# A two-layer graph attention kernel in which DMAs add up part of each softmax denominator, and the second layer's norms run in whole-chunk steps

## The chip, the cores and the metric

One core of one Trainium2 chip runs the whole kernel in one launch. The metric is device time in microseconds (us) of one execution, lower is better. Five engines matter: TensorE (PE in the profile; PEld is its weight load), VectorE (DVE), ScalarE (ACT), GpSimd (POOL) and SyncE (SP), which here only issues DMAs. Each engine works through its own queue in order; an instruction that waits holds everything behind it on that engine.

## The reference

Input `x` is 8 graphs x 2048 nodes x 64 features in f32, and `adj` is one 2048 x 2048 matrix of 0 and 1 that all graphs share. Two attention layers run over it, and a residual layer norm ends it:

```python
def _gat_layer(h, mask, b):                       # h: [..., N, D]
    scores = einsum('...nd,...md->...nm', h, h)
    scores = where(mask, scores, -1e16)
    return einsum('...nm,...md->...nd', softmax(scores), h) + b

mask = graph + eye(N) > 0
h    = einsum('bnc,hdc->bhnd', x, Wh)             # 4 heads of 64
z    = leaky_relu(cat(_gat_layer(h, mask, bh)), 0.2)
h2   = einsum('bnk,dk->bnd', z, Wo)               # one head of 64
z2   = leaky_relu(_gat_layer(h2, mask, bo), 0.2)
out  = (z2 - mean) * rsqrt(var + 1e-5) * gamma + beta
x    = layernorm(x + out)
```

## The kernel before

`fast_kernel` does all the work. (`general_kernel` stands behind a flag for inputs whose exponentials leave a safe range; it is not executed here.)

**Units, chunks, blocks.** A unit is one attention over two 64-row maps at once (`j` = 0, 1: two heads of one graph in the first layer, two graphs in the second). There are 20 units: 16 of the first layer and 4 of the second. A second-layer unit (`self.second`) comes when the first-layer units that feed it are done: two of them stand in between first-layer units, two come at the end. A unit has `NC` = 4 chunks of `W` = 512 columns, and a chunk has `NB` = 16 blocks `m` of 128 rows. A step `t` of the main loop is one block, so 1,280 steps in all, 1,024 of the first layer and 256 of the second.

**One block.** `scores` makes a 128 x (2 x 512) block of scores on TensorE in PSUM (two buffers), VectorE subtracts the mask from it into an SBUF tile `e`, and ScalarE takes exp in place. Three steps later (`LAG` = 3) `values` multiplies `e` by the features on TensorE, accumulated over the 16 blocks in PSUM tile `o`. Each f32 matmul shows as two MATMUL records in the profile.

**The denominators.** They are the column sums of all 16 `e` blocks of a chunk. `add_up` hands blocks to GpSimd, which adds them to an SBUF tile `acc`, in the order of blocks. The last `DIRECT` blocks (3 in the first layer, 7 in the second) are not added up but kept as they are. So a first-layer chunk has 4 terms (`acc` and 3 blocks), a second-layer chunk 8. `sums` lets TensorE end them: each term is multiplied by a column of ones for `j` = 0 and 1, and half of the terms go to another column group of the array than the other half. ScalarE copies the result (`zsb`), four small DMAs lay it out over partitions (`zt`), `invert` takes the reciprocal on VectorE, and DMAs bring it back as a 128 x 512 tile `z` by way of DRAM (`rd`). `scale` multiplies.

**The norms.** `norm` does the two layer norms of a second-layer chunk in parts 0 to 7. ScalarE copies and squares the result (part 0), VectorE reduces (1), GpSimd takes the power -1/2 and scales, applies gamma and beta and adds x (2, 3), VectorE reduces (4), ScalarE squares the eight groups of 64 columns one by one with an accumulated sum (5), GpSimd takes the power (6), and ScalarE scales the eight groups one by one (7), after which SyncE stores.

**What sets the order.** The order is written out by hand: `steps` is the list of blocks, `jobs` holds what is done after step `t`, and two tables give the step of each late part of a chunk, counted from its first block: `LATE` for the denominators and `NORM` for parts 0 to 7. Pieces of one chunk therefore stand between blocks of the next ones. `slot` hands out 13 SBUF tiles for the `e` blocks; a tile comes free when its readers are done. Tiles of tag `w` (six) hold `oj`, `o5`, `zsb`, `z`, `sq`; tag `y` (three) holds the norms' `y` and `xr`.

Of the kernel before, what the change touches and what calls it, by code (L numbers as in the profile page):

```python
# [24 lines left out]
F32 = mybir.dt.float32  # L29
# [3 lines left out]
AF = mybir.ActivationFunctionType  # L33
OP = mybir.AluOpType
AX = mybir.AxisListType
# [320 lines left out]
def fast_kernel(ctx: ExitStack, tc: tile.TileContext, x, adj, Wh, bh, Wo, bo, gamma, beta, out, flag):  # L356

    nc = tc.nc
    B, N, C = x.shape
    H, D, _ = Wh.shape  # L360
    P = 128
    NB = N // P
    W = 512
# [14 lines left out]
    dram = ctx.enter_context(tc.tile_pool(name="scratch", bufs=4, space=bass.MemoryType.DRAM))  # L378
# [11 lines left out]
    def wtile(name):  # L390
        return work.tile([P, W], F32, tag="w", name=name)

    def ytile(name):
        return work.tile([P, W], F32, tag="y", name=name, bufs=3)


    ident = const.tile([P, P], F32, name="ident")
# [12 lines left out]
    shifts = const.tile([P, 4], F32, name="shifts")  # L410
# [4 lines left out]
    mhalf = const.tile([P, K], F32, name="mhalf")  # L415
# [94 lines left out]
    class Unit:  # L510


        def __init__(self, n, bp, b2, hp):
            self.n, self.bp, self.b2, self.hp = n, bp, b2, hp
            self.second = hp is None
            self.terms, self.zt, self.z, self.O = {}, {}, {}, {}

        def prepare(self, h):

# [33 lines left out]
        def add_up(self, c, m, e):  # L553

            if m == 0:
                self.terms[c] = [e]
            elif m == 1:
                acc = accs.tile([P, 2, W], F32, tag="acc", name=f"acc{self.n}_{c}")
                nc.gpsimd.tensor_tensor(acc, self.terms[c][0], e, OP.add)  # L559
                self.terms[c] = [acc]  # L560
            elif m < NB - DIRECT[self.second]:
                acc = self.terms[c][0]
                nc.gpsimd.tensor_tensor(acc, acc, e, OP.add)  # L563
            else:
                self.terms[c].append(e)


        def join(self, c):
# [41 lines left out]
        def invert(self, c):  # L610
            n = self.n
            k = n * NC + c
            nc.vector.tensor_reduce(zall[:, k, :], self.zt.pop(c).rearrange("p s k -> p k s"), AX.X, OP.add)
            rt = small.tile([P, 8], F32, tag="rt", name=f"rt{n}_{c}")
            nc.vector.reciprocal(rt, zall[:, k, :])
            rd = dram.tile([2, W], F32, tag="rd", name=f"rd{n}_{c}")
            nc.sync.dma_start(out=rd.rearrange("j (p k) -> (j p) k", k=8), in_=rt)
            self.z[c] = wtile(f"z{n}_{c}")
            for j in range(2):
                nc.sync.dma_start(out=self.z[c][j * D:(j + 1) * D, :], in_=rd[j].partition_broadcast(D))  # L620

# [32 lines left out]
        def norm(self, c, part):  # L654
            if not self.second:
                return
            n = self.n
            v = lambda t: t.rearrange("p (k d) -> p k d", d=D)
            row = lambda t: t.unsqueeze(1).to_broadcast([P, K, D])
            col = lambda t: t.unsqueeze(2).to_broadcast([P, K, D])  # L660
            if part == 0:
                self.y = ytile(f"y{n}_{c}")
                nc.scalar.copy(self.y, self.O[c][0])
                self.sq = wtile(f"sq{n}_{c}")
                nc.scalar.square(self.sq, self.O[c][0])
                self.xr = ytile(f"xr{n}_{c}")
                xv = self.xr.rearrange("p (i b d) -> p i b d", b=2, d=D)
                for b2 in range(2):
                    nc.sync.dma_start(out=xv[:, :, b2, :],
                                      in_=x[2 * self.bp + b2, c * W:(c + 1) * W, :].rearrange("(i p) d -> p i d", p=P))  # L670
                return
            y, xr = self.y, self.xr
            if part == 1:
                self.st = small.tile([P, 6, K], F32, tag="st", name=f"st{n}_{c}", bufs=2)
                nc.vector.tensor_reduce(self.st[:, 0, :], v(self.sq), AX.X, OP.add)
            st = self.st
            if part == 2:
                nc.scalar.activation(st[:, 1, :], st[:, 0, :], AF.Identity, bias=shifts[:, 3:4], scale=1.0 / D)  # L678
                nc.gpsimd.tensor_tensor(st[:, 0, :], st[:, 1, :], mhalf, OP.pow)  # L679
                nc.gpsimd.tensor_tensor(v(y), v(y), col(st[:, 0, :]), OP.mult)  # L680
            elif part == 3:
                nc.gpsimd.tensor_tensor(v(y), v(y), row(gam), OP.mult)
                nc.gpsimd.tensor_tensor(v(y), v(y), row(bet), OP.add)
                nc.gpsimd.tensor_tensor(y, y, xr, OP.add)
            elif part == 4:
                nc.vector.tensor_reduce(st[:, 2, :], v(y), AX.X, OP.add)
            elif part == 5:
                nc.scalar.mul(st[:, 3, :], st[:, 2, :], -1.0 / D)
                for k in range(K):
                    nc.scalar.activation(v(xr)[:, k, :], v(y)[:, k, :], AF.Square, bias=st[:, 3, k:k + 1], scale=1.0,  # L690
                                         accum_out=st[:, 4, k:k + 1])
            elif part == 6:
                nc.scalar.activation(st[:, 5, :], st[:, 4, :], AF.Identity, bias=shifts[:, 3:4], scale=1.0 / D)
                nc.gpsimd.tensor_tensor(st[:, 0, :], st[:, 5, :], mhalf, OP.pow)  # L694
                nc.gpsimd.tensor_tensor(st[:, 1, :], st[:, 3, :], st[:, 0, :], OP.mult)  # L695
            elif part == 7:
                for k in range(K):
                    nc.scalar.activation(v(xr)[:, k, :], v(y)[:, k, :], AF.Identity, bias=st[:, 1, k:k + 1],  # L698
                                         scale=st[:, 0, k:k + 1])
                yv = xr.rearrange("p (i b d) -> p i b d", b=2, d=D)  # L700
# [48 lines left out]
    for i, k in enumerate(range(done, len(pieces) + AHEAD + 1)):  # L749
# [1 line left out]
    xst = {}  # L751


    LATE = [(19, "join"), (20, "join2"), (20, "sums"), (21, "fifth"), (22, "leaky"), (24, "invert"), (28, "scale"), (30, "project"),
            (31, "keep")]
    NORM = [31, 32, 33, 35, 40, 41, 43, 46]
    es = {}
    for t in range(total + 64):
        if t < total:
            u, c, m = steps[t]  # L760
            es[t] = u.scores(c, m)
            if m == 0:
# [5 lines left out]
                n = u.n + 1  # L768
                if n < len(units):
                    v = units[n]  # L770
# [13 lines left out]
        if 0 <= t - LAG < total:  # L784
            u, c, m = steps[t - LAG]
            e = es.pop(t - LAG)
# [57 lines left out]
```

## Time and profile before

| | |
|---|---|
| three runs | 2678.69 us median (2677.74 to 2680.65) |
| profiled execution | 2678.89 us, of which 2677.1 us from the first to the last instruction (the span) |
| TensorE clock granted, mean | 0.985 |
| TensorE busy | 2580.8 us (96%) |
| GpSimd busy | 2265.1 us (85%) |
| VectorE busy | 1832.5 us (68%) |
| ScalarE busy | 1783.3 us (67%) |
| DMA | 55.40 MB, a mean of 21 GB/s |

A busy share is an average over stages with different limits, so the stages are looked at one by one. A row of the timeline gives start, duration, engine, line, operation, tiles (out<-in) and how many instructions are merged in it; in square brackets stands the time that the engine sat idle before it and what ended the wait. A row of a group gives line, engine, operation, tiles, shape and count, then total busy us and mean ns of one, then idle us before them. L563 is line 563 of the kernel before.

### The profile page before, as it was taken

How to read it: one execution, taken by the hardware profiler on the slowest of the kernel's cores; microseconds unless marked ns; L12 is line 12 of the kernel's file. 1: busy time of each engine (PE TensorE's matmuls, PEld its weight loads, DVE VectorE, ACT ScalarE, POOL GpSimd, SP SyncE). 2: the span in 40 equal slices, each digit the busy share in tenths (PEclk: the TensorE clock that was granted, in tenths of full speed). 3: DMA queues.
4: the chain of work that ended last, by engine and by line, in shares of the span. 5: the costliest groups of instructions: out<-in, count | busy, mean ns of one | idle time of the engine just before them, and what ended most of it. 6: DMA issues, size and time to landing. Idle time of an engine off the chain costs nothing.

```text
span 2677.1 us, 54824 instructions
## 1 busy us (share of the span) xinstructions
PE 2580.8 (96%) x23174; PEld 896.5 (33%) x23174; DVE 1832.5 (68%) x1797; ACT 1783.3 (67%) x2089; POOL 2265.1 (85%) x1041
## 2 busy tenths in 40 slices
PE   7999999999999999999999899999999999999993
PEld 3333333333333233333333233333333333333331
DVE  5876776677766577667776667767776777766662
ACT  5766666666667666666667766666666666666774
POOL 5889999899688999889967989988998999967774
PEclk9999999999999999999999999999999999999996
DMA  5300001000001001000001000100000000000011
GB/s 143 125 25 10 9 9 25 10 14 10 13 17 25 9 14 25 10 10 10 10 14 25 21 9 10 25 9 14 9 9 10 10 10 13 10 13 17 21 25 29
DMA packets 118304, 55.40 MB, mean 21 GB/s; under 512 B 91266, under 2 KB 107714, under 8 KB 118050
## 3 DMA queue, kind: packets, MB, share of 16 engines
q1 hardware_dynamic: 117250, 51.36, 7.2%
q8 instruction: 183, 3.00, 0.5%
q0 software_dynamic: 176, 0.26, 0.1%
q14 instruction: 71, 0.58, 0.1%
q10 hardware_dynamic: 624, 0.20, 0.0%
HBM read 46.60 MB, written 4.52 MB: 19 GB/s over the span
## 4 chain that ended last, share of the span: by engine, by line
PE 76%; POOL 11%; ACT 6%; DVE 3%; issue 3%; DMA 0%; SPq 0%; POOLq 0%; DVEq 0%; ACTq 0%
PE s L537 34%; PE o L550 33%; POOL acc L563 6%; PE pz L597 5%; ACT e L541 3%; DVE e L540 2%; PE pn L527 1%; ACT xr L698 1%; PE o L641 1%; ACT xr L690 1%; POOL acc L559 1%; POOL st L694 1%; POOL st L679 1%; ACT hT L508 1%; PE pm L484 1%
## 5 line engine op out<-in xcount | busy, mean ns | idle before, releaser
L540 DVE TENSOR_TENSOR e<-s,mask 128x1024 f32<-128x1024 f32 x1280 | 1562.6, 1222 | 721.7 <-PE s L537 700.3
L563 POOL TENSOR_TENSOR acc<-acc,e 128x1024 f32<-128x1024 f32 x816 | 1933.5, 2369 | 81.2 <-ACT e L541 20.2
L541 ACT ACTIVATE e<-e,shifts 128x1024 f32<-128x1024 f32 x1280 | 1465.1, 1148 | 762.5 <-DVE e L540 748.4
L550 PE MATMUL o<-e,hN 64*64 64x512 f32 x10240 | 1336.6, 592 | 20.2 <-ACT e L541 20.1
L537 PE MATMUL s<-hT 64*64 64x512 f32 x8192 | 1074.3, 595 | 9.6 <-DVE e L540 4.5
L550 PEld LDWEIGHTS o<-e,hN 64*64 64x64 f32 x10240 | 390.9, 134 | 738.6 <-issue 540.7
L537 PEld LDWEIGHTS s<-hT 64*64 64x64 f32 x8192 | 295.8, 133 | 582.2 <-issue 424.9
L559 POOL TENSOR_TENSOR acc<-e,e 128x1024 f32<-128x1024 f32 x80 | 189.3, 2367 | 139.5 <-ACT e L541 139.2
L537 PE MATMUL s<-h2T 64*64 64x512 f32 x2048 | 273.1, 604 | 15.7 <-DVE e L540 15.6
L597 PE MATMUL pz<-e,ones 128*32 128x512 f32 x1216 | 182.1, 600 | 0.0
L679 POOL TENSOR_TENSOR st<-st,mhalf 128x8 f32<-128x8 f32 x16 | 26.3, 1641 | 127.3 <-ACT st L678 127.3
L537 PEld LDWEIGHTS s<-h2T 64*64 64x64 f32 x2048 | 75.2, 135 | 157.9 <-issue 121.3
L597 PE MATMUL pz<-acc,ones 128*32 128x512 f32 x320 | 85.0, 610 | 0.1
L600 ACT COPY zsb<-pz 128x512 f32<-128x512 f32 x80 | 46.7, 584 | 48.3 <-PE pz L597 48.3
L698 ACT ACTIVATE xr<-y,st 128x64 f32<-128x64 f32 x128 | 44.1, 426 | 42.8 <-POOL st L695 42.8
L597 PEld LDWEIGHTS pz<-e,ones 128*32 128x32 f32 x1216 | 41.0, 110 | 68.5 <-issue 68.5
L585 DVE TENSOR_TENSOR o<-o,o 128x512 f32<-128x512 f32 x80 | 55.8, 698 | 5.2 <-ACT o L581 5.2
L624 DVE TENSOR_TENSOR z<-o,z 128x512 f32<-128x512 f32 x80 | 54.5, 681 | 6.0 <-DMA z<-rd 5.7
L577 DVE TENSOR_TENSOR o<-o,oj 128x512 f32<-128x512 f32 x80 | 55.9, 698 | 2.4 <-ACT oj L572 1.0
L485 DVE CAST mask<-pm 128x1024 uint8<-128x1024 bf16 x32 | 39.1, 1223 | 18.5 <-PE pm L484 16.6
L581 ACT ACTIVATE o<-o 128x512 f32<-128x512 f32 x80 | 46.2, 577 | 0.0
L572 ACT COPY oj<-o 128x512 f32<-128x512 f32 x80 | 45.6, 569 | 0.4
(74 smaller groups left out, 681.8 us busy)
## 6 DMA issues: line engine op xcount, KB each, us to landing
z<-rd SPq DMA_DIRECT2D x160, 128.0 KB, 2.9
adj<-in_adj_dram SPq DMA_DIRECT2D x32, 512.0 KB, 4.8
zt<-zsb SPq DMA_DIRECT2D x320, 2.0 KB, 1.8
x<-in_x_dram SPq DMA_DIRECT2D x16, 256.0 KB, 4.6
xr<-in_x_dram SPq DMA_DIRECT2D x32, 128.0 KB, 2.7
out_dram<-xr SPq DMA_DIRECT2D x32, 128.0 KB, 2.1
rd<-rt SPq DMA_DIRECT2D x80, 4.0 KB, 1.4
ws<-in_L_gnn_Wh_dram ACTq DMA_DIRECT2D x2, 64.0 KB, 4.6
```

Of the source, the lines that this page charges most:

```text
L537: nc.tensor.matmul(ps[k * 64:(k + 1) * 64, j, :], self.hT[rows, m * P + k * 64:m * P + (k + 1) * 64], self.hT[rows, c * W:(c + 1) * W], st ...
L540: nc.vector.tensor_tensor(e, ps, mask[c][:, m, :].unsqueeze(1).to_broadcast([P, 2, W]), OP.subtract)
L541: nc.scalar.activation(e, e, AF.Exp, bias=shifts[:, 1:2] if self.second else shifts[:, 0:1], scale=1.0)
L550: nc.tensor.matmul(self.O[c][r][j * D:(j + 1) * D, :], self.hN[rows, m, j * D:(j + 1) * D], e[rows, j, :], start=(m == 0), stop=(m == NB - 1))
L559: nc.gpsimd.tensor_tensor(acc, self.terms[c][0], e, OP.add)
L563: nc.gpsimd.tensor_tensor(acc, acc, e, OP.add)
L577: nc.vector.tensor_tensor(b, b, self.t, OP.add)
L585: nc.vector.tensor_tensor(b, b, self.t, OP.max)
L597: nc.tensor.matmul(pz[q:q + 32, :W], ones, terms[s * half + k][:, j, :], start=(k == 0), stop=(k == half - 1), tile_position=(0, q))
L624: nc.vector.tensor_tensor(dst, self.O[c][1], self.z[c], OP.mult)
L679: nc.gpsimd.tensor_tensor(st[:, 0, :], st[:, 1, :], mhalf, OP.pow)
L698: nc.scalar.activation(v(xr)[:, k, :], v(y)[:, k, :], AF.Identity, bias=st[:, 1, k:k + 1], scale=st[:, 0, k:k + 1])
```

## The change

`add_up` no longer gives all blocks to GpSimd's adder. By the table `CHAINS`, some blocks are added by DMAs issued from GpSimd's queue that read a block and add it onto an earlier block in SBUF (`accum_op=OP.add`). In a first-layer chunk, blocks 3, 6, 9 and 12 are added one after the other onto block 0 (five blocks in one term). In a second-layer chunk, blocks 4, 8, 12 go onto block 0 and blocks 6, 10, 14 onto block 2. GpSimd adds the others into `acc`, now the last blocks too, except block 15 of a second-layer chunk, which stays alone. That leaves 2 terms in the first layer and 4 in the second.

The norms become ten parts: the second norm uses the steps of the first one (GpSimd subtracts the mean, ScalarE squares a whole chunk, VectorE reduces, GpSimd takes the power and scales) in place of the sixteen small ScalarE instructions. `LATE` and `NORM` move most parts by one step or more, and `sums` from behind `join2` to behind `fifth`. Tag `w` has three tiles, `y` four, and `z` gets two of its own.

```diff
-    DIRECT = (3, 7)
+    CHAINS = (((0, 3, 6, 9, 12),), ((0, 4, 8, 12), (2, 6, 10, 14)))
+    ALONE = ((), (15,))
-    work = ctx.enter_context(tc.tile_pool(name="work", bufs=6))
+    work = ctx.enter_context(tc.tile_pool(name="work", bufs=3))
...
         def add_up(self, c, m, e):
             if m == 0:
-                self.terms[c] = [e]
-            elif m == 1:
+                self.terms[c], self.first, self.acc = [], {}, None
+            for k, chain in enumerate(CHAINS[self.second]):
+                if m == chain[0]:
+                    self.first[k] = e
+                    self.terms[c].append(e)
+                    return
+                if m in chain:
+                    nc.gpsimd.dma_start(out=self.first[k], in_=e, accum_op=OP.add)
+                    return
+            if m in ALONE[self.second]:
+                self.terms[c].append(e)
+            elif self.acc is None:
+                self.acc = e
+            elif len(self.terms[c]) == len(CHAINS[self.second]):
                 acc = accs.tile([P, 2, W], F32, tag="acc", name=f"acc{self.n}_{c}")
-                nc.gpsimd.tensor_tensor(acc, self.terms[c][0], e, OP.add)
-                self.terms[c] = [acc]
-            elif m < NB - DIRECT[self.second]:
-                acc = self.terms[c][0]
-                nc.gpsimd.tensor_tensor(acc, acc, e, OP.add)
+                nc.gpsimd.tensor_tensor(acc, self.acc, e, OP.add)
+                self.acc = acc
+                self.terms[c].append(acc)
             else:
-                self.terms[c].append(e)
+                nc.gpsimd.tensor_tensor(self.acc, self.acc, e, OP.add)
...
             elif part == 5:
-                nc.scalar.mul(st[:, 3, :], st[:, 2, :], -1.0 / D)
-                for k in range(K):
-                    nc.scalar.activation(v(xr)[:, k, :], v(y)[:, k, :], AF.Square, bias=st[:, 3, k:k + 1], scale=1.0,
-                                         accum_out=st[:, 4, k:k + 1])
+                nc.scalar.mul(st[:, 4, :], st[:, 3, :], -1.0 / D)
+                nc.gpsimd.tensor_tensor(v(y), v(y), col(st[:, 4, :]), OP.add)
             elif part == 6:
-                nc.scalar.activation(st[:, 5, :], st[:, 4, :], AF.Identity, bias=shifts[:, 3:4], scale=1.0 / D)
-                nc.gpsimd.tensor_tensor(st[:, 0, :], st[:, 5, :], mhalf, OP.pow)
-                nc.gpsimd.tensor_tensor(st[:, 1, :], st[:, 3, :], st[:, 0, :], OP.mult)
-            elif part == 7:
-                for k in range(K):
-                    nc.scalar.activation(v(xr)[:, k, :], v(y)[:, k, :], AF.Identity, bias=st[:, 1, k:k + 1],
-                                         scale=st[:, 0, k:k + 1])
+                self.sq = wtile(f"sr{n}_{c}")
+                nc.scalar.square(self.sq, y)
...
-    NORM = [31, 32, 33, 35, 40, 41, 43, 46]
+    NORM = [32, 33, 34, 36, 42, 43, 45, 46, 47, 50]
```

Parts 7 and 8 are now the reduce of part 1 and the power and scale of part 2 again, and part 9 stores. Three places show how instructions move. A name such as `e_1_3_1873` is block 3 of chunk 1 (the last number only tells buffers apart); names in brackets are what the instruction waits for: `DMASW` is a DMA issued by GpSimd, `DMAHW` one issued by SyncE, the others are engines.

GpSimd's queue in a first-layer chunk, before: one add for each block.

```order
L559 TENSOR_TENSOR acc_1_1902<-e_1_0_1843,e_1_1_1855 128x1024 [waits Activation_49]
L563 TENSOR_TENSOR acc_1_1902<-acc_1_1902,e_1_2_1867 128x1024 [waits Activation_49,Pool_49]
L563 TENSOR_TENSOR acc_1_1902<-acc_1_1902,e_1_3_1879 128x1024 [waits Activation_49,Pool_49]
L563 TENSOR_TENSOR acc_1_1902<-acc_1_1902,e_1_4_1895 128x1024 [waits Activation_49,Pool_49]
L563 TENSOR_TENSOR acc_1_1902<-acc_1_1902,e_1_5_1926 128x1024 [waits Activation_49,Pool_49]
```

The same queue and chunk now.

```order
L573 TENSOR_TENSOR acc_1_1909<-e_1_1_1847,e_1_2_1860 128x1024 [waits Activation_49]
L565 DMA e_1_0_1834<-e_1_3_1873 128x1024 [waits DMAHW1_49,DMAHW2_49,PE_49,Activation_49]
L577 TENSOR_TENSOR acc_1_1909<-acc_1_1909,e_1_4_1889 128x1024 [waits Activation_49,Pool_49]
L577 TENSOR_TENSOR acc_1_1909<-acc_1_1909,e_1_5_1902 128x1024 [waits Activation_49,Pool_49]
L565 DMA e_1_0_1834<-e_1_6_1930 128x1024 [waits DMASW1_49,Activation_49]
L577 TENSOR_TENSOR acc_1_1909<-acc_1_1909,e_1_7_1944 128x1024 [waits Activation_49,Pool_49]
L577 TENSOR_TENSOR acc_1_1909<-acc_1_1909,e_1_8_1957 128x1024 [waits Activation_49,Pool_49]
L565 DMA e_1_0_1834<-e_1_9_1970 128x1024 [waits DMASW2_49,Activation_49]
```

Every third block is a DMA, and from the second one on it waits in GpSimd's queue for the landing of the one before it, two adds earlier.

TensorE's queue where it ends the denominators of a first-layer chunk (`pz`), before.

```order
L597 MATMUL pz_0_2903<-acc_0_2662,ones 32x512 x2
L597 MATMUL pz_0_2903<-e_0_14_2815,ones 32x512 x2
L597 MATMUL pz_0_2903<-e_0_13_2802,ones 32x512 x2
L597 MATMUL pz_0_2903<-e_0_15_2828,ones 32x512 x2
L537 MATMUL s_1_5_2919<-hT_1_2100 64x512 x4
```

The same place now.

```order
L552 MATMUL o_1_1_2867<-e_1_2_2850,hN_2352 64x512
L609 MATMUL pz_0_2903<-e_0_0_2588,ones 32x512 x2
L609 MATMUL pz_0_2903<-acc_0_2663,ones 32x512 x2
L539 MATMUL s_1_6_2915<-hT_1_2091 64x512 x4
L552 MATMUL o_1_0_2866<-e_1_3_2863,hN_2352 64x512
```

Four of eight matmuls are gone, and the place is one block later (before `s_1_6` instead of `s_1_5`).

ScalarE's queue at the end of a second-layer chunk's norms, before (`st`, `xr`, `y` of chunk 0 between the exponentials of chunk 2).

```order
L693 ACTIVATE st_0_6093<-st_0_6093,shifts 128x8 [waits Activation_49]
L541 ACTIVATE e_2_12_6300<-e_2_12_6300,shifts 128x1024 [waits DVE_49]
L541 ACTIVATE e_2_13_6313<-e_2_13_6313,shifts 128x1024 [waits DVE_49]
L541 ACTIVATE e_2_14_6325<-e_2_14_6325,shifts 128x1024 [waits DVE_49]
L698 ACTIVATE xr_0_6078<-y_0_6074,st_0_6093 128x64 [waits Pool_49]
L698 ACTIVATE xr_0_6078<-y_0_6074,st_0_6093 128x64 x7
L541 ACTIVATE e_2_15_6351<-e_2_15_6351,shifts 128x1024 [waits DVE_49]
```

The same place now.

```order
L700 ACTIVATE st_0_6049<-st_0_6049 128x8
L543 ACTIVATE e_2_12_6240<-e_2_12_6240,shifts 128x1024 [waits DVE_49]
L543 ACTIVATE e_2_13_6253<-e_2_13_6253,shifts 128x1024 [waits DVE_49]
L704 ACTIVATE sr_0_6261<-y_0_6045 128x512 [waits Pool_49]
L543 ACTIVATE e_2_14_6269<-e_2_14_6269,shifts 128x1024 [waits DVE_49]
L543 ACTIVATE e_2_15_6283<-e_2_15_6283,shifts 128x1024 [waits DMASW1_49,DVE_49,Activation_49]
L690 ACTIVATE st_0_6049<-st_0_6049,shifts 128x8
```

ScalarE still waits for GpSimd once per chunk, now at one squaring (`sr`), and behind one short GpSimd step instead of behind the power.

More of the change, by code (lines that the diff above doesn't have):

```diff
@@ L393, in ytile @@
     def ytile(name):
[L394 removed]
+        return work.tile([P, W], F32, tag="y", name=name, bufs=4)
     ident = const.tile([P, P], F32, name="ident")
@@ L751, in fast_kernel @@
     xst = {}
-    LATE = [(19, "join"), (20, "join2"), (20, "sums"), (21, "fifth"), (22, "leaky"), (24, "invert"), (28, "scale"), (30, "project"),
-            (31, "keep")]
-    NORM = [31, 32, 33, 35, 40, 41, 43, 46]
+    LATE = [(19, "join"), (20, "join2"), (21, "fifth"), (21, "sums"), (22, "leaky"), (25, "invert"), (29, "scale"), (31, "project"),
+            (32, "keep")]
+    NORM = [32, 33, 34, 36, 42, 43, 45, 46, 47, 50]
     es = {}
```

25 lines of the change are left out of this document (13 added, 12 removed).

## Prediction

> **What bounds the kernel now.** I read the page's busy shares first, then TensorE by stage, then the chain of waits, then the groups by line.
>
> ```profile
> span 2677.1 us, 54824 instructions
> PE 2580.8 (96%) x23174; PEld 896.5 (33%) x23174; DVE 1832.5 (68%) x1797; ACT 1783.3 (67%) x2089; POOL 2265.1 (85%) x1041
> PE 76%; POOL 11%; ACT 6%; DVE 3%; issue 3%; DMA 0%; SPq 0%; POOLq 0%; DVEq 0%; ACTq 0%
> ```
>
> The stages, as busy times in windows (start:end, length, then busy us of each engine, granted clock, DMA share, GB/s):
>
> ```profile
> core 0: us, PE busy (x) PEld busy (x) DVE busy (x) ACT busy (x) POOL busy (x), PEclk, DMA share, GB/s
> 40.00:140.00 100.00, 99.96 (x948) 37.01 (x940) 86.57 (x80) 78.44 (x75) 84.54 (x43) 1.00 0.39 120
> 300.00:640.00 340.00, 339.74 (x3072) 116.38 (x3068) 239.89 (x233) 226.39 (x221) 309.06 (x131) 1.00 0.06 13
> 737.00:900.00 163.00, 149.42 (x1312) 50.44 (x1304) 99.89 (x102) 114.29 (x203) 140.44 (x74) 0.97 0.08 19
> 1390.00:1555.00 165.00, 151.25 (x1328) 51.11 (x1324) 101.90 (x104) 115.12 (x202) 143.12 (x75) 0.97 0.08 19
> 2420.00:2640.00 220.00, 202.72 (x1748) 68.80 (x1740) 132.43 (x137) 152.34 (x285) 165.22 (x92) 0.95 0.09 23
> ```
>
> In a first-layer stage (300 to 640) TensorE has no idle time, at full clock: what leaves its queue there shortens the run, as long as GpSimd, busy 309 of 340 us, doesn't become the limit. In the three second-layer stages TensorE idles 13.6, 13.8 and 17.3 us and its clock falls to 0.97 and 0.95. Why, the timeline of one such place shows:
>
> ```profile
> 875.33 1.65 POOL L694 TENSOR_TENSOR st<-st,mhalf 128x8 f32<-128x8 f32 x1
> 877.29 2.76 ACT L698 ACTIVATE xr<-y,st 128x64 f32<-128x64 f32 x8 [6.34 <-POOL st L695]
> 879.95 2.17 ACT L541 ACTIVATE e<-e,shifts 128x1024 f32<-128x1024 f32 x2
> 881.14 1.56 PE L550 MATMUL o<-e,hN 64*64 64x512 f32 x8 [4.94 <-ACT e L541]
> ```
>
> ScalarE stood 6.3 us before the norm's last scaling, since GpSimd reached the power (L694) late, behind its adds. The exponentials queued behind it came late, and TensorE waited 4.9 us, then ran its eight records in 1.56 us where 1.04 is usual (below).
>
> **The change, part by part.**
>
> *TensorE ends fewer terms.* The two groups of `pz` count 1,536 records, 16 in each of 64 first-layer chunks and 32 in each of 16 second-layer chunks.
>
> ```profile
> L597 PE MATMUL pz<-e,ones 128*32 128x512 f32 x1216 | 182.1, 600 | 0.0
> L597 PE MATMUL pz<-acc,ones 128*32 128x512 f32 x320 | 85.0, 610 | 0.1
> 1330.83 1.46 PE L597 MATMUL pz<-e,ones 128*32 128x512 f32 x10
> 1332.21 1.09 PE L537 MATMUL s<-h2T 64*64 64x512 f32 x8
> 1333.12 1.04 PE L550 MATMUL o<-e,hN 64*64 64x512 f32 x8
> 1333.98 1.04 PE L537 MATMUL s<-h2T 64*64 64x512 f32 x8
> ```
>
> They become 8 and 16, so 768 go. A mean of 600 ns is no price, since records overlap; from start to start, eight take 1333.98 - 1333.12 = 0.86 us, 0.107 each, and a block of 16 takes 1.72. The ten `pz` records above took 1.38 us, 0.138 each, with the change of tile shape, which stays. So 768 x 0.107 = 82 us (by the other price 106), nearly all where TensorE never idles. I take 82.
>
> *GpSimd.* Per first-layer chunk 12 adds become 10 adds and 4 DMA issues, per second-layer chunk 8 become 6 and 6.
>
> ```profile
> 997.75 12.16 POOL L563 TENSOR_TENSOR acc<-acc,e 128x1024 f32<-128x1024 f32 x5
> 1.64 0.74 POOL L454 DMA_DIRECT2D bhb<-in_L_gnn_bh_dram  x1
> 3.97 0.53 POOL L458 DMA_DIRECT2D bet<-in_L_gnn_beta_dram  x1
> ```
>
> An add takes 12.16/5 = 2.43 us, so ten take 24.3. The only DMAs that GpSimd issues before cost it 0.53 to 0.74 us each; each has 128 rows, as the new ones have, so I take 0.65 = d, with bounds 0.5 and twice 0.74 (two operands). The chunk is then 24.3 + 2.6 = 26.9 us of GpSimd. TensorE's chunk: 131 adds in 340 us are 10.9 chunks of 31.1 us, less 0.86 is 30.3; the shortest, 16 x 1.72 and 0.9, is 28.4. GpSimd has room in both.
>
> *The new wait.* DMA k+1 of a chain waits, in GpSimd's queue, for the landing of DMA k; in between stand two adds (4.86 us). If issue to landing takes L, the chunk costs GpSimd 24.3 + d + 3 max(d, L - 4.86); behind the waiting DMA stand all later adds, and `sums` on TensorE waits for the last of them. This stays under 30.3 us up to L = 6.6, and eats up all that the change gains at L = 7.2. No row shows an accumulating transfer. The nearest:
>
> ```profile
> adj<-in_adj_dram SPq DMA_DIRECT2D x32, 512.0 KB, 4.8
> zt<-zsb SPq DMA_DIRECT2D x320, 2.0 KB, 1.8
> z<-rd SPq DMA_DIRECT2D x160, 128.0 KB, 2.9
> bhb<-in_L_gnn_bh_dram POOLq DMA_DIRECT2D x1, 128.0 KB, 4.9
> bet<-in_L_gnn_beta_dram POOLq DMA_DIRECT2D x1, 32.0 KB, 9.1
> ```
>
> `adj` moves as many bytes over as many partitions, so 4.8 is the lower bound. `zt`, within SBUF, has hardly any bytes; 4.8 - 1.8 = 3.0 is then the moving, and twice that for two operands gives 7.8, the upper bound. GpSimd's own DMAs land later (4.9 for 128 KB where SyncE's `z` takes 2.9; 9.1 for the last in line), but in the loading at the start. I take L = 5.5, `adj` and d, nearest to the row of its size: then GpSimd waits for nothing in the first layer. The Trainium skill, in DMA: Bandwidth & Descriptors, "Anatomy of one DMA — SWDGE (gpsimd) path", has 2.0 us and bytes / 436 GB/s for a DMA from GpSimd; my estimate from it is 3.2 us for 512 KB, less than `adj` took here, and by it the 7 us below that I charge for late landings would go.
>
> *What the transfers disturb.* 352 of them, 512 KB each. In window 40 to 140, at a DMA share of 0.39, TensorE is busy 99.96 of 100, so its cost is none. The way of `z` is tighter:
>
> ```profile
> 1024.65 1.10 SPq L620 DMA_DIRECT2D z<-rd  x2
> 1029.61 0.68 DVE L624 TENSOR_TENSOR z<-o,z 128x512 f32<-128x512 f32 x1
> ```
>
> The second is issued at 1025.2 and lands 2.9 later; VectorE uses it 1.5 us after that. If sharing queues doubled the landing, it would be 1.4 us late 80 times, of which 0.5 lies in VectorE's slack per block (1.72 against 1.22): 72 us. Between 0 and 72 I take 5, since the row gives room for half as long again. Slots: a chunk's first block is held to step 21, so two of 13 at most, where three last blocks were held; eight blocks or more (14 us) pass before a transfer's source is written again. Cost none. Tag `w` with three tiles: a fourth is asked for 14 steps after the first, long after its reader; in the mask's stage ScalarE may wait for it, 0 to 10 us, I take none.
>
> *The norms.* GpSimd's part of a chunk, by these rows:
>
> ```profile
> L679 POOL TENSOR_TENSOR st<-st,mhalf 128x8 f32<-128x8 f32 x16 | 26.3, 1641 | 127.3 <-ACT st L678 127.3
> L680 POOL TENSOR_TENSOR y<-y,st 128x512 f32<-128x512 f32 x16 | 16.7, 1042 | 1.3
> L684 POOL TENSOR_TENSOR y<-y,xr 128x512 f32<-128x512 f32 x16 | 20.4, 1274 | 1.3
> L540 DVE TENSOR_TENSOR e<-s,mask 128x1024 f32<-128x1024 f32 x1280 | 1562.6, 1222 | 721.7 <-PE s L537 700.3
> L698 ACT ACTIVATE xr<-y,st 128x64 f32<-128x64 f32 x128 | 44.1, 426 | 42.8 <-POOL st L695 42.8
> ```
>
> Two powers (1.64), three of 1.04 (scale twice, subtract the mean) and three of 1.28, with gaps 10.8 us, where it was 9. A second-layer chunk takes 6 x 2.43 + 6 x 0.65 + 10.8 = 29.3 us of GpSimd, TensorE 16 x 1.72 + 1.7 + 1.1 (the centring matmuls) = 30.3: it fits, and GpSimd alternates adds and issues where it ran eight adds on end, so ScalarE's one wait (`sr`) should find it in time. What was lost there before: 44.6 us idle and, by the clocks (0.03 x 328 + 0.05 x 220 = 21, of which I count 13, as some of it lies in the idle time), 58 in all. What is late next: block 14's DMA is issued some 5 us before TensorE reaches `sums`, so 0.6 us in each of 12 chunks, 7. And twice, norms of a second-layer unit run in two first-layer chunks, which need 24.3 + 2.6 + 10.8 = 37.7 us of GpSimd against 30.3: 2 x 7.4, less 3 us that `sums` has in hand, is 12, twice 24. So 58 - 31 = 27 gained, between -10 and 58. SyncE's queue has the same DMAs, the store three steps later; nobody waits for it before the end. At the end the tail gets 2 us shorter (half the `pz`, two groups of eight like L698's 2.76 us gone, one wait for block 14 more), between -4 and +3.
>
> **The sum.** The profiled execution took 2678.89 us, 1.8 more than its span and 0.2 over the median of the runs (2678.69). 2678.9 - 82 - 27 - 2 + 5 = 2573.
>
> **The rivals.**
>
> A, slower: the adding transfer takes 7.2 us or more, and GpSimd's chain is the bound. For it speaks that it reads two operands and that GpSimd's DMAs landed latest of all; against it that `adj` at 4.8 was measured in the busiest stage of the DMA queues. At 7.8 the chunk is 24.3 + 0.65 + 8.8 = 33.8, 3.5 over 30.3, x 64 = 224: 2797. At 7.5 it is 2737. The Trainium skill, in Collectives: The Full Stack, "The bandwidth ceiling: the fold count and why AG ≠ RS ≠ AR", says that an adding transfer pushes two reads through one read ring and gets half the rate of a copy. That is this case's mechanism; no run here shows it yet.
>
> B, slower: the issue itself costs GpSimd over 1.9 us (24.3 + 4d = 32.0). At three times the 0.74 row it gives 33.2, 2.9 x 64 = 186: 2759. Against it: two to three times any row.
>
> C, less gained: the waits only move. The norms' stalls come back as waits for the last landing, and `z` comes late: 2573 + 27 + 67 = 2667, down to 2630 for half of it. For it speaks the 1.5 us in hand; against it that GpSimd no longer runs eight adds on end.
>
> D, no change: TensorE isn't short of time where `pz` stands. Against it stands 339.74 of 340.
>
> **How the numbers follow.** This kernel's runs spread by 0.1%, so 0.2% is about what can be told from no change. Forecast 0.58 (2540 to 2630: from all 58 us of stalls gained to `z` half late), C 0.12, D 0.04, A 0.20, B 0.06. Faster is the forecast and C, 0.70; same is D, 0.04; slower is A and B, 0.26. The likeliest is 2573. For 8 in 10 the range goes from 2540 to 2740, up to L = 7.5: half of A, most of B and a little below are left out. Within the forecast alone it is 2540 to 2630.
>
> **What would show it.** `pz` groups with 768 records in all; `add` groups with 736; in window-like first-layer stages TensorE still without idle time and GpSimd busy under 95%. The issue of an accumulating DMA under 0.8 us, its landing under 6.6. In the second layer, idle time of TensorE about half of what it was, and ScalarE's wait before `sr` under 2 us. Wrong would be: GpSimd idle before its DMA with the DMA as releaser, 64 x 3 times; TensorE waiting for `acc` or for the chain's block at `pz`; a granted clock under 0.98 in the first layer, which an idle TensorE would bring; VectorE waiting at L624's place for `z`.

## The result, and the profile after

The change made the kernel faster: 2605.49 us median (2604.9 to 2612.93, 4 runs) against 2678.22 of the kernel before beside it (2676.3 to 2680.65, 4 runs), a ratio of 0.9734, 95% interval 0.9715 to 0.9754. That is 73 us, where 106 were forecast. A second set of runs gave 0.9725 (0.9711 to 0.9738). The span of the profiled execution is 2604.0 us.

The page of the changed kernel, its busy shares and its chain of waits:

```profile
span 2604.0 us, 53831 instructions
...
PE 2507.1 (96%) x22406; PEld 866.4 (33%) x22406; DVE 1834.2 (70%) x1813; ACT 1703.5 (65%) x1721; POOL 2214.6 (85%) x1249
...
PE 67%; DMA 9%; POOL 5%; DVE 5%; issue 3%; ACT 3%; SPq 1%; DVEq 0%; ACTq 0%; POOLq 0%
```

768 matmul records are gone, but DMA, which had 0% of the chain before, now has 9%. The windows, at the same kinds of place as before (the loading, a first-layer stretch, the three second-layer stretches; their places moved with the shorter span):

```profile
core 0: us, PE busy (x) PEld busy (x) DVE busy (x) ACT busy (x) POOL busy (x), PEclk, DMA share, GB/s
40.00:140.00 100.00, 95.28 (x873) 34.48 (x872) 81.30 (x75) 75.07 (x71) 78.49 (x47) 0.97 0.72 178
300.00:640.00 340.00, 336.24 (x3012) 114.03 (x3008) 241.25 (x235) 227.18 (x223) 295.41 (x154) 1.00 0.42 81
730.00:890.00 160.00, 149.66 (x1320) 51.36 (x1312) 107.48 (x113) 101.97 (x117) 146.33 (x91) 0.98 0.47 92
1370.00:1530.00 160.00, 151.61 (x1324) 51.16 (x1320) 107.93 (x112) 101.97 (x115) 148.89 (x93) 0.98 0.47 94
2370.00:2580.00 210.00, 190.89 (x1696) 67.89 (x1688) 141.59 (x151) 131.22 (x157) 186.52 (x128) 0.96 0.59 117
```

TensorE, which had no idle time in the first layer (339.74 of 340) and none in the loading (99.96 of 100), now idles 3.8 and 4.7 us there, at DMA shares of 0.42 and 0.72 where 0.06 and 0.39 were. Groups of instructions show for what:

```profile
L577 POOL TENSOR_TENSOR acc<-acc,e 128x1024 f32<-128x1024 f32 x656 | 1605.5, 2447 | 129.8 <-ACT e L543 104.7
...
L565 POOL DMA_DIRECT2D e<-e x352 | 320.7, 911 | 48.6 <-ACT e L543 25.4
...
L609 PE MATMUL pz<-e,ones 128*32 128x512 f32 x448 | 100.1, 610 | 10.1 <-DMA e<-e 7.2
L636 DVE TENSOR_TENSOR z<-o,z 128x512 f32<-128x512 f32 x80 | 54.9, 687 | 72.1 <-DMA z<-rd 72.0
L609 PE MATMUL pz<-acc,ones 128*32 128x512 f32 x320 | 85.0, 610 | 9.4 <-POOL acc L577 9.4
...
e<-e POOLq DMA_DIRECT2D x352, 512.0 KB, 4.9
z<-rd SPq DMA_DIRECT2D x160, 128.0 KB, 3.6
adj<-in_adj_dram SPq DMA_DIRECT2D x32, 512.0 KB, 7.8
zt<-zsb SPq DMA_DIRECT2D x320, 2.0 KB, 1.8
```

The accumulating DMA itself is no bottleneck: 0.91 us of GpSimd to issue, 4.9 us to landing. But `z` lands in 3.6 us where 2.9 was, and VectorE waits 72 us for it at the scale (L636), 40 times. Before, the row of the scale was:

```profile
L624 DVE TENSOR_TENSOR z<-o,z 128x512 f32<-128x512 f32 x80 | 54.5, 681 | 6.0 <-DMA z<-rd 5.7
```

One such wait in the timeline of the changed kernel:

```profile
603.51 0.69 DVE L636 TENSOR_TENSOR z<-o,z 128x512 f32<-128x512 f32 x1 [2.48 <-DMA z<-rd]
...
604.12 2.34 DVE L542 TENSOR_TENSOR e<-s,mask 128x1024 f32<-128x1024 f32 x2
605.36 2.33 ACT L543 ACTIVATE e<-e,shifts 128x1024 f32<-128x1024 f32 x2 [3.09 <-DVE e L542]
605.38 1.09 PE L539 MATMUL s<-hT 64*64 64x512 f32 x8 [1.36 <-DVE e L542]
```

VectorE stands 2.48 us before the scale; the mask's subtraction (L542) queued behind it is late, so the score buffers come free late, and TensorE idles 1.36 us.

Where the 73 us lie, by stretches of the span. Each stretch is cut where ScalarE copies a chunk's sums (`zsb`); "start" is the time to the first score matmul, when the kernel only loads. One profiled execution each, in us:

| stretch (chunks) | before | changed | chains alone | norms alone | gap | gap+later | relief | mixed |
|---|---|---|---|---|---|---|---|---|
| start | 28.7 | 25.7 | 29.6 | 29.9 | 30.4 | 29.7 | 27.4 | 31.6 |
| loading (first 4) | 151.1 | 158.9 | 156.2 | 151.1 | 152.3 | 151.8 | 152.2 | 152.5 |
| first layer, three stretches (56) | 1753.0 | 1727.3 | 1727.4 | 1753.0 | 1715.0 | 1714.5 | 1716.4 | 1716.5 |
| second layer, first place (6) | 211.5 | 200.2 | 204.7 | 214.0 | 206.2 | 200.6 | 194.6 | 196.5 |
| second layer, second place (6) | 211.4 | 202.5 | 201.3 | 214.6 | 202.1 | 200.0 | 191.8 | 192.9 |
| second layer, at the end (8) | 282.2 | 252.0 | 258.4 | 280.9 | 253.8 | 255.3 | 262.1 | 255.0 |
| tail | 39.2 | 37.4 | 39.6 | 38.1 | 38.1 | 37.9 | 42.4 | 42.9 |

The columns behind "changed" are the experiments below (the profiled execution of "gap" was 8 us over its median). In the first layer, the time from the first `pz` record to the next other matmul, added up, fell from 103.8 to 55.8 us, 48.0, though the stretch got only 25.7 shorter.

### The profile page after: what moved, and what is told of

It is laid out like the page before. It is cut to its first block, busy times and chain, and to the rows that moved or that the text cites. A ratio compares the mean times of both kernels' runs of the same rounds, so it can differ in the third digit from the quotient of the medians.

```text
span 2604.0 us, 53831 instructions
## 1 busy us (share of the span) xinstructions
PE 2507.1 (96%) x22406; PEld 866.4 (33%) x22406; DVE 1834.2 (70%) x1813; ACT 1703.5 (65%) x1721; POOL 2214.6 (85%) x1249
## 3 DMA queue, kind: packets, MB, share of 16 engines
q0 software_dynamic: 50864, 184.83, 37.8%
## 4 chain that ended last, share of the span: by engine, by line
PE 67%; DMA 9%; POOL 5%; DVE 5%; issue 3%; ACT 3%; SPq 1%; DVEq 0%; ACTq 0%; POOLq 0%
PE s L539 32%; PE o L552 29%; DVE e L542 4%; DMA z<-rd 4%; PE pz L609 3%; POOL acc L577 3%; DMA rd<-rt 2%; DMA e<-e 2%; DMA zt<-zsb 1%; PE pn L529 1%; ACT e L543 1%; PE o L653 1%; POOL st L691 1%; SPq L618 1%; POOL y L692 1%
## 5 line engine op out<-in xcount | busy, mean ns | idle before, releaser
L542 DVE TENSOR_TENSOR e<-s,mask 128x1024 f32<-128x1024 f32 x1280 | 1558.8, 1221 | 588.6 <-PE s L539 566.6
L577 POOL TENSOR_TENSOR acc<-acc,e 128x1024 f32<-128x1024 f32 x656 | 1605.5, 2447 | 129.8 <-ACT e L543 104.7
L539 PEld LDWEIGHTS s<-hT 64*64 64x64 f32 x8192 | 289.9, 133 | 611.5 <-issue 378.5
L565 POOL DMA_DIRECT2D e<-e x352 | 320.7, 911 | 48.6 <-ACT e L543 25.4
L609 PE MATMUL pz<-e,ones 128*32 128x512 f32 x448 | 100.1, 610 | 10.1 <-DMA e<-e 7.2
L636 DVE TENSOR_TENSOR z<-o,z 128x512 f32<-128x512 f32 x80 | 54.9, 687 | 72.1 <-DMA z<-rd 72.0
L691 POOL TENSOR_TENSOR st<-st,mhalf 128x8 f32<-128x8 f32 x32 | 56.9, 1777 | 41.6 <-ACT st L690 41.4
L531 DVE TENSOR_TENSOR hN<-pn,bhb 128x1024 f32<-128x1024 f32 x32 | 39.1, 1223 | 8.6 <-PE pn L529 7.8
```

The costliest lines, as they stand in the source:

```text
L539: nc.tensor.matmul(ps[k * 64:(k + 1) * 64, j, :], self.hT[rows, m * P + k * 64:m * P + (k + 1) * 64], self.hT[rows, c * W:(c + 1) * W], st ...
L542: nc.vector.tensor_tensor(e, ps, mask[c][:, m, :].unsqueeze(1).to_broadcast([P, 2, W]), OP.subtract)
L565: nc.gpsimd.dma_start(out=self.first[k], in_=e, accum_op=OP.add)
L577: nc.gpsimd.tensor_tensor(self.acc, self.acc, e, OP.add)
L609: nc.tensor.matmul(pz[q:q + 32, :W], ones, terms[s * half + k][:, j, :], start=(k == 0), stop=(k == half - 1), tile_position=(0, q))
L636: nc.vector.tensor_tensor(dst, self.O[c][1], self.z[c], OP.mult)
```

## The experiments

**What each half of the change is worth.** The first kernel has the chains with the norms of before (`norm` as it was, `NORM = [32, 33, 34, 36, 41, 42, 44, 47]`); the second has the new norms without the chains:

```diff
-    CHAINS = (((0, 3, 6, 9, 12),), ((0, 4, 8, 12), (2, 6, 10, 14)))
-    ALONE = ((), (15,))
+    CHAINS = ((), ())
+    ALONE = ((13, 14, 15), (9, 10, 11, 12, 13, 14, 15))
```

> The denominators' part alone; the norms are the kernel before's, with their parts one step later as the rest of the table asks. Theory: the norms' new steps gave about 16 us, read from the end of the kernel (the two last second-layer units became 30.2 us shorter, of which 8 chunks x 1.72 us are the missing pz records), and nothing in the two second-layer units in the middle; so this kernel takes 2605 + 16 = 2621 us (2613 to 2632), and the waits of ScalarE for GpSimd's st are back (over 25 us). Rival 1, the prediction's size: the norms gave 27 to 58 us, so 2632 or more. Rival 2: the chain's shorter rows of adds cured the norm stalls by themselves, so the norms' edit gave nothing: 2605.

> The norms' part alone (with the new late tables and tiles); the denominators are summed as before, 4 and 8 terms, no accumulating DMA, sums back at step 20. Theory: the norms' edit gives about 16 us, so 2662 us (2652 to 2670); z lands in 2.9 us again, adj in 4.8, and VectorE waits under 10 us for z, because no transfer disturbs them. Rival 1: the late tables, not the transfers, made z late: VectorE's waits for z stay above 40 us here too. Rival 2: the norm steps need the lighter GpSimd queue of the chains, and with eight adds on end the norms are no faster: 2678.

Chains alone: 2614.4 us, 0.9753 (0.9739 to 0.9766). Norms alone: 2684.53 us against 2681.2, 1.0014 (1.0005 to 1.0023): no gain, and 1 to 6 us lost. So the theory failed for the second kernel, and its second rival held. The first kernel's time lies in its theory's range (2613 to 2632), but the sign of that theory, waits of over 25 us, did not come. ScalarE's waits for GpSimd, in three rows from the waits of norms alone, chains alone and the changed kernel (line awaited, total us, times, longest):

```profile
ACT sr L704 <- POOL y L701: 79.4, 16, 9.0
```
```profile
ACT xr L710 <- POOL st L707: 9.4, 4, 3.0
```
```profile
ACT sr L704 <- POOL y L701: 12.4, 6, 5.9
```

In the kernel before that wait was 42.8 us. The new norms give GpSimd one step more (the mean), and behind eight adds on end they make ScalarE wait 79.4. The chains cure the wait by themselves: 9.4 us with the old norms. Between chains alone (0.9753) and the changed kernel (0.9734 and 0.9725) lie 5 to 8 us, which the norms' edit adds to them. And with the late tables of the change, but no transfers (only `sums` is back at step 20), `z` is not late in norms alone:

```profile
L636 DVE TENSOR_TENSOR z<-o,z 128x512 f32<-128x512 f32 x80 | 54.5, 681 | 5.7 <-DMA z<-rd 5.7
...
z<-rd SPq DMA_DIRECT2D x160, 128.0 KB, 3.0
```

**Whether transfers in flight make `z` late.** One row of numbers changes. `z` of a chunk is fetched between the next chunk's blocks 7 and 10 or so (the step of a block's DMA is the block plus 3); the other chain leaves that time free, with as many DMAs and adds.

```diff
-    CHAINS = (((0, 3, 6, 9, 12),), ...
+    CHAINS = (((0, 1, 4, 10, 13),), ...
```

> One number row changed: a first-layer chain is blocks 0, 1, 4, 10, 13 instead of 0, 3, 6, 9, 12. As many DMAs and adds, but none of the DMAs is issued between step 7 and step 13 of a chunk, which is when the z tile of the chunk before is fetched. Theory (an accumulating transfer in flight slows the fetch of z, and late z costs TensorE some 22 us of the first layer): median landing of z falls from 3.6 to about 3.0 us, VectorE's wait at the scale from 72 to under 25 us, and the time is 2583 to 2592 us. Rival 1 (z is late for the tables' sake): waits and time as they are, 2605. Rival 2 (the waits are real but TensorE loses its time elsewhere): waits fall, time within 3 us of 2605. Against the change: up to five adds stand in a row, and GpSimd may be late for the block behind: then pz<-acc waits appear.

2591.16 us, 0.9664 (0.9651 to 0.9677), so 16 to 19 us less than the changed kernel's two ratios. Its groups:

```profile
L636 DVE TENSOR_TENSOR z<-o,z 128x512 f32<-128x512 f32 x80 | 54.6, 683 | 29.3 <-DMA z<-rd 29.1
...
z<-rd SPq DMA_DIRECT2D x160, 128.0 KB, 3.0
...
zt<-zsb SPq DMA_DIRECT2D x320, 2.0 KB, 3.4
```

`z` lands in 3.0 again and the wait fell to 29, a little over the 25 expected. Fetch by fetch, for the 139 of 160 whose landing is on record: in the changed kernel 124 overlapped with an accumulating transfer for 2 us or more, and their median landing was 3.85 us, the longest 6.0; here 94 had no overlap and took 2.91, and 34 had 2 us or more, and took 3.95. The gain lies where the waits were: loading 6.6 us and first layer 12.3. What had been in the way moved: `zt`, the step before, now lands in 3.4 us instead of 1.8, at the place where block 1's DMA now flies.

**The same wait, relieved from the other side.**

```diff
-    LATE = [..., (29, "scale"), (31, "project"), (32, "keep")]
-    NORM = [32, 33, 34, 36, 42, 43, 45, 46, 47, 50]
+    LATE = [..., (30, "scale"), (32, "project"), (33, "keep")]
+    NORM = [33, 34, 35, 37, 43, 44, 46, 47, 48, 51]
```

> Scale, project, keep and all norm parts one step later (30, 32, 33 and 33 to 51), all else as in the changed kernel. z has 1.9 us more to land. Theory (late z costs the first layer some 22 us): VectorE's wait at the scale falls from 72 to under 15 us, the landing of z stays at 3.6, and the time is 2583 to 2592 us. Rival 1 (the waits cost TensorE nothing): the wait falls and the time stays at 2605 within 3 us. Rival 2: the later release of the PSUM tile o, asked for again at step 35, makes TensorE wait at the first value product of a chunk: 1 us in each of 64 chunks at worst, so up to 2650.

2599.06 us, 0.9698 (0.9685 to 0.9711), 7 to 10 us less than the changed kernel, half of what was expected. Its groups:

```profile
L636 DVE TENSOR_TENSOR z<-o,z 128x512 f32<-128x512 f32 x80 | 54.7, 684 | 17.4 <-DMA z<-rd 17.0
...
z<-rd SPq DMA_DIRECT2D x160, 128.0 KB, 3.8
```

The transfers still stretch `z`, and one step more covers most of it. In the second layer other waits grew: TensorE waited at `pz` 12.3 us for `acc` and 12.5 for the last transfers, where the changed kernel had 9.4 and 7.2. The edits together:

> Both single edits together: chain 0, 1, 4, 10, 13 and the late parts from scale on one step later. Theory (both work on the same wait): VectorE's wait at the scale is under 8 us, and the ratio to the kernel before is a little under that of the chain alone (0.966): 0.962 to 0.965, some 2580 us; it does not fall by the sum of both (0.963 - 0.004). Rival (each of them gains by something of its own): 0.9625 or less, with the scale's wait not near zero. Rival 2: the later release of the PSUM tile takes back what the waits give: 0.967 or more.

2594.19 us, 0.9671 (0.9657 to 0.9684): the wait is 12.8 us, and there is no gain over the gap alone, against what was expected. By the ratio the second rival held, but its mechanism doesn't show: no wait of TensorE at a value product for the tile `o` is among its waits. In the first-layer window TensorE is whole again:

```profile
L636 DVE TENSOR_TENSOR z<-o,z 128x512 f32<-128x512 f32 x80 | 54.6, 682 | 12.8 <-DMA z<-rd 12.8
```
```profile
300.00:640.00 340.00, 339.38 (x3048) 116.76 (x3040) 244.82 (x239) 229.99 (x226) 299.04 (x155) 1.00 0.41 81
```

Its first layer is 38.5 us shorter than before, where `pz` gives 47.1 (103.8 to 56.7). Of the missing 9 us, 5.5 lie at one place: one step behind `pz`, a block's value product takes 0.96 us to the next product, where it took 0.86 before (means of 56 chunks, from start to start). The profile names no wait there; it names none under 0.15 us. Why this is so stays open.

**What an accumulating transfer costs.** In four units of the first layer TensorE gets 8 terms and GpSimd adds 8 blocks; three of the units also write dead tiles:

```diff
+                if m in (2, 5, 8) and self.n == 13:
+                    nc.gpsimd.dma_start(out=self.dead, in_=e)
+                elif m in (2, 5, 8) and self.n == 14:
+                    nc.gpsimd.dma_start(out=self.dead, in_=e, accum_op=OP.add)
+                elif m in (2, 5, 8) and self.n == 15:
+                    nc.gpsimd.dma_start(out=self.dead[:, 0, :], in_=e[:, 0, :], accum_op=OP.add)
```

> One look at the price of the transfer itself. The changed kernel, but in four units of the first layer (the 13th to the 16th in order) GpSimd adds 8 blocks and 8 terms go to TensorE, with no transfer in the first of them; in the next three, three transfers per chunk (after blocks 2, 5 and 8) write a tile that is no longer read: plain copies of 512 KB in the second unit, accumulating ones of 512 KB in the third, accumulating ones of 256 KB in the fourth. Theory (adding costs the DMA engines a second read, and that is what stretches z): plain copies land in about 3 to 3.5 us and leave z's landing near 2.9 to 3.1; accumulating ones land in 4.9 and stretch z to 3.5 or more; 256 KB accumulating land in about 3.4 (halfway to the 1.8 of the smallest). Rival (any transfer of 512 KB from GpSimd's queue costs the same): plain copies land in 4.7 or more and stretch z as much as the accumulating ones. GpSimd's issue: 0.9 us for all if it is set by the rows, about half for a plain copy if by the second operand.

One execution, and windows over the units with plain copies (1712 to 1842 us), with accumulating ones (1848 to 1972), and with those of half the size. Queue rows give packets, MB and the share of 16 engines; issue rows the landing; group rows busy us and mean ns.

```profile
q0 software_dynamic: 1528, 5.54, 10.8%
...
e<-e POOLq DMA_DIRECT2D x11, 512.0 KB, 2.9
...
L585 POOL DMA_DIRECT2D e<-e x10 | 5.7, 567 | 5.5 <-PE o L552 4.4 <-ACT e L543 1.1
```
```profile
q0 software_dynamic: 1691, 5.99, 25.6%
...
e<-e POOLq DMA_DIRECT2D x11, 512.0 KB, 4.6
...
L587 POOL DMA_DIRECT2D e<-e x11 | 9.6, 873 | 1.9 <-PE o L552 1.5 <-PE s L539 0.4
```
```profile
e<-e POOLq DMA_DIRECT2D x11, 256.0 KB, 3.3
```

A plain copy of 512 KB lands in 2.9 us and costs GpSimd 0.57; adding makes it 4.6 and 0.87. For the DMA engines, 25.6% of 124 us for 5.99 MB is 5.3 us a MB, and 10.8% of 130 us for 5.54 MB is 2.5: 2.1 times. By the rule of the Trainium skill that the prediction set under rival A (Collectives: The Full Stack, "The bandwidth ceiling: the fold count and why AG ≠ RS ≠ AR", told there of the reduce step of a collective: two reads through one read ring, half the rate), this would be a factor of two; the trace agrees with the factor. The Trainium skill's rule in DMA: Bandwidth & Descriptors, "Anatomy of one DMA — SWDGE (gpsimd) path", 2.0 us and bytes / 436 GB/s (3.2 us as an estimate for 512 KB), fits the plain copy's 2.9 and not the adding one's 4.6. The expectation for `z` missed: its landing stayed at 2.8 us beside the accumulating transfers. In that unit only one of eight fetches overlapped one by 2 us, so this run hardly tests it. In the unit with plain copies one fetch overlapped a copy by 2.5 us and took 3.57: whether a transfer must add in order to stretch `z` stays open.

**Where GpSimd is short.** The kernel called relief builds on gap+later. The two chunks behind each second-layer unit in the middle are summed in the second layer's way, and the second layer's chains are moved so that they leave `z`'s time free too (the lines against the changed kernel, without the late tables):

```diff
-    CHAINS = (((0, 3, 6, 9, 12),), ((0, 4, 8, 12), (2, 6, 10, 14)))
+    CHAINS = (((0, 1, 4, 10, 13),), ((0, 4, 10, 13), (1, 5, 11, 14)))
...
+        def kind(self, c):
+            return int(self.second or (self.n in (6, 11) and c < 2))
```

The kernel called mixed gives the two last units the changed kernel's two chains back.

> As the kernel with both single edits; the second layer's two chains become 0, 4, 10, 13 and 1, 5, 11, 14, which also leave the time of z's fetch free, and the two chunks after each second-layer unit in the middle, which carry its norms on GpSimd, are summed in the second layer's way (6 adds, 6 DMAs, 4 terms). Theory (there GpSimd is short of time: 10 adds, 4 issues and the norms are some 39 us against 30, and TensorE waits 9.4 us for acc and 7.2 for the last transfers): waits of pz for acc fall under 3 us, the two middle second-layer stretches become 5 us shorter each, and the ratio is 0.003 to 0.005 under the kernel with both edits. Rival (the transfers of two chains disturb z and each other more than the adds cost): no gain within 0.1%, e<-e landing over 5.5 us.

> As the relieved kernel (chain 0, 1, 4, 10, 13, late parts one step later, relief after the two middle second-layer units), but the two last units have the changed kernel's two chains (0, 4, 8, 12 and 2, 6, 10, 14) back. Theory (in the last stretch TensorE waited 21.7 us at pz for the last transfer, because chains that end with blocks 13 and 14 land too late there): the last stretch goes from 262 to about 254 us, the tail from 42 to 38, the ratio from 0.9654 to 0.961 or 0.962. Rival (those waits only replaced others): 0.965, unchanged.

Relief: 2588.72 us, 0.9654 (0.964 to 0.9667), 0.0017 under gap+later, where 0.003 to 0.005 was expected. The two places got 6.0 and 8.2 us shorter than in gap+later, as expected, and TensorE no longer waits for `acc`; but the last stretch got 6.8 longer, since two chains that end with blocks 13 and 14 land late. The tail got 4.5 longer too, for another reason: from the issue of the last DMA, the flag's, to the end it is 11.9 us instead of 8.1, behind all chains. TensorE's waits in relief, and in mixed:

```profile
PE pz L612 <- DMA e<-e: 21.7, 12, 6.0
```
```profile
PE pz L614 <- DMA e<-e: 17.5, 10, 4.6
```

Mixed: 2588.24 us, 0.9651 (0.9638 to 0.9664). Its last stretch came back from 262 to 255 as expected, but not the tail (42.9, of it 12.2 behind the last DMA's issue), so the chains were not what lengthened the tail; what did stays open. The time is relief's, not the 0.961 expected: in the profiled execution the start took 4.2 us more. Both beat the kernel before and the changed one, by 3.5% and 0.8%.

**The loading.** Relief, with the first unit summed without accumulating DMAs (`CHAINS` empty, `ALONE` 13, 14, 15 there).

> As the relieved kernel, and the first unit, in which adj is loaded, is summed without accumulating DMAs (12 adds, 4 terms). Theory (the transfers stretched the loads: adj from 4.8 to 7.8 us, and the loading part lost some 8 us of which pz gave 3.4 back): adj lands in about 5 us, the loading part takes 181 to 182 us instead of 183 to 185, ratio 0.0005 to 0.001 lower. Rival (the load is bound by something else): loading part and time unchanged, or slower by the 3.4 us of pz.

2590.73 us, 0.9661 (0.9648 to 0.9675): no gain. `adj` lands in 5.6 us instead of 6.1, and nobody had waited for it. That theory of the loading falls: what the loading lost in the changed kernel was the same late `z`. In the window 40 to 140 TensorE was busy 95.28 of 100 in the changed kernel; in relief, with as many transfers at other times, and in this kernel without any:

```profile
40.00:140.00 100.00, 99.03 (x936) 36.75 (x932) 86.73 (x80) 78.72 (x75) 80.57 (x48) 1.00 0.70 180
```
```profile
40.00:140.00 100.00, 99.95 (x950) 36.52 (x943) 86.46 (x79) 79.23 (x75) 85.29 (x43) 1.00 0.39 122
```

**The norms with the chains in place.** Mixed, with the kernel before's norms.

> As the mixed kernel, with the kernel before's norms (their parts two steps later than there). It prices the norms' edit with the chains in place. Theory (the chains gave GpSimd back in time and so cured most of the norm stalls; ScalarE's 16 small instructions cost TensorE little): 3 to 8 us slower than the mixed kernel, a ratio 0.001 to 0.003 higher. Rival, the prediction's size: 27 us, 0.010 higher. Rival 2: no difference, or faster, as the norms alone were 3 us slower without the chains.

> The changed kernel once more, unaltered, on the chip of the mixed kernel, so that the two ratios stand against the same runs of the kernel before: 0.9734 again, within 0.002; the mixed kernel is then 30 us shorter.

2597.45 us, 0.9687 (0.9673 to 0.97), 9.2 us more than mixed: the norms' edit is worth that much, a little over what was expected, once the chains have made GpSimd's queue short. The changed kernel again took 2608.18, its ratio as expected; so mixed is 20 us shorter, not the expected 30.

## Why the prediction was right or wrong

*Fewer terms: right.* 768 records by 0.107 us made 82. The first layer's `pz` time alone fell by 48.0, and 56 chunks x 8 x 0.107 is 47.9.

*GpSimd and the new wait: right, with both sizes off.* The issue took 0.91 us, not 0.65 (a plain copy of that size took 0.57); the landing 4.9, not 5.5. The lower bound of 4.8, from `adj`, did not hold: 4.6 was measured among few transfers, and 2.9 for a plain copy. Before its DMAs, GpSimd waited 10.8 us in all for the landing of an earlier one:

```profile
POOL e L565 <- DMA e<-e: 10.8, 10, 2.7
```

That is nothing of what rival A asked for, and in the first-layer window GpSimd is busy 295.41 of 340, 87%. At 0.91 an issue, rival B fell too.

*What the transfers disturb: here the prediction failed.* It took 5 us between 0 and 72 for a late `z`, and nothing for the loading. It had the 1.5 us in hand and both bounds, but took a value near the lower one, since the row gave room for half as long again. For the loading it went by TensorE's 99.96 of 100, which shows what plain loads cost the products, and not what more transfers do to `z`. In place of 5: loading +7.8 though `pz` gave 3.4 there (4 chunks x 0.86), so 11.2; first layer 48.0 - 25.7 = 22.3. Together 33.5 us. The gap kernel, with as many transfers at other times, gave 6.6 and 12.3 of it back, so 19 are shown to be the late `z`. The other 14.6 are not: some 9 stay in the first layer even in gap+later, where `z` is nearly in time, most of them behind `pz`, with their cause open. The mechanism was named right (VectorE waiting at L624's place), its size was not. A chain that issues every third block has an accumulating transfer in flight through most of `z`'s fetch (4.9 us every 5.2), so `z` meets one nearly always (124 of 139 fetches for 2 us or more), not sometimes.

*The norms: right in sign, too large, and due in half to the chains.* -27 was forecast, because GpSimd would no longer run eight adds on end. That is the chains' doing. The second-layer stretches got 11.2 + 8.9 + 30.2 = 50.3 shorter; `pz` is 31 of it (16 chunks x 1.72 and 4 x 0.86), so 19.3 is the term's measure. Half of it comes with the chains alone (40.7 shorter), which leave GpSimd's queue shorter at the norms; the edit of the norms gives 5 to 8 beside the same chains, 9 in mixed, and -3 without chains. ScalarE's wait before `sr` (12.4 us, the longest 5.9) isn't under 2. TensorE's idle time in the three second-layer windows was to halve; it went from 44.6 us of 548 to 37.8 of 530, late `z` included. The late landing and the busy transitions were foreseen as 7 and 24; TensorE waited 7.2 for the last transfers and 9.4 for `acc`, and relief won 14 back.

*The tail* was forecast at -2 and came to -1.8; the start was 3.0 shorter, which varies from 25.7 to 31.6 between executions of kernels that do the same there, and was 29.2 in the second profile of the changed kernel: that is luck.

The sum: -82.4 + 11.2 + 22.3 - 19.3 - 1.8 - 3.0 = -73.0, and 2677.1 - 73.0 = 2604.1. The terms are read off the stretches, so the sum must close; of them, the 19 us of the late `z` and the two halves of the norms' 19.3 rest on experiments of their own. The outcome lies inside the forecast's own range (2540 to 2630), whose upper end stood for `z` half late. Rival C named both waits that came.

## What to carry to other kernels

Before work is given to DMAs, ask which small transfer stands on the critical path while they fly: here the late 128 KB behind a 1.5 us margin cost 19 us that could be had back, while TensorE waited only 7.2 us for the 352 transfers themselves. If it is late, move the big transfers out of its time first (a row of block numbers gave 16 to 19 us); more time for it gave 7 to 10 by itself, and nothing on top. And price two edits to one queue together: the norms' edit lost 3 us alone and gave 5 to 9 once the queue in front of it was shorter.

## What the runs showed of the hardware

A stall of TensorE can cost about twice its length. In the kernel with the gap VectorE waited 4.42 us for one fetch of `z`, and TensorE idled 3.30 us. Timeline, and windows before and behind it (granted clock third from the end; the last window is the stretch at half clock):

```profile
690.67 0.69 DVE L636 TENSOR_TENSOR z<-o,z 128x512 f32<-128x512 f32 x1 [4.42 <-DMA z<-rd]
...
692.55 1.99 PE L539 MATMUL s<-h2T 64*64 64x512 f32 x8 [3.30 <-DVE e L542]
...
694.31 1.93 PE L552 MATMUL o<-e,hN 64*64 64x512 f32 x8
```
```profile
680.00:688.00 8.00, 8.00 (x80) 2.91 (x76) 5.15 (x6) 5.21 (x5) 7.36 (x6) 1.00 0.77 145
692.00:699.00 7.00, 6.45 (x36) 1.96 (x40) 3.78 (x4) 3.42 (x3) 0.88 (x1) 0.54 0.39 75
691.66:698.49 6.83, 5.94 (x28) 1.79 (x32) 3.61 (x4) 3.42 (x3) 0.88 (x1) 0.50 0.40 77
```

Eight records took 1.93 to 1.99 us instead of 1.04, at a granted clock of 0.50, for about 6 us: 3 us lost behind 3.3 us of waiting. The Trainium skill, in TensorE: Matmul & The Clock Gate, "Part 1: The HAM clock gate (the "warmup" mystery)", has the array fall to half speed after an idle window of about 3.4 us and come back after a busy one, in windows that run on whatever the kernel does. The trace agrees with the way back: half clock stood for 6.83 us, two such windows, and only through the second of them was TensorE busy without a break. The fall came sooner than by that rule, at 691.66, 2.4 us after TensorE's last product ended (689.25). The stalls of 1 to 1.4 us in the first layer left the clock at 1.00.
